# Expert blocks of a mixture layer, laid out over four rounds instead of two

## The chip, the cores and the metric

The kernel runs on one core of a Trainium2 chip. It is one launch of a program in which every engine has its own stream of instructions: TensorE (PE, with its weight loads shown apart as PEld), VectorE (DVE), ScalarE (ACT), GpSimd (POOL) and SyncE (SP). PE does the matrix products, DVE, ACT and POOL the rest of the arithmetic, and SP and POOL issue DMA transfers. Each engine works through its stream in order, and engines wait for each other by semaphores. The metric is the device time of one execution in microseconds, as the median of several runs. All data are 32-bit floats.

## The reference

Four layers are computed on a residual `x` of 4 sequences of 1024 tokens with 128 channels. Every layer has the shape "half a feed-forward step, an attention step, half a feed-forward step". Layers 0 and 2 use a mixture of 8 experts, of which each token takes its best two. Layer 0, cut to what matters (layer 2 has the same form with ReLU, and takes its softmax over the two kept logits):

```python
logits = jnp.einsum('td,ed->te', xf, router_w)
top_vals, top_idx = jax.lax.top_k(logits, K)          # K = 2 of 8 experts
probs = jax.nn.softmax(top_vals, axis=-1)
for e in range(E):
    w = jnp.sum(jnp.where(top_idx == e, probs, 0.0), axis=-1)
    h = jax.nn.gelu(jnp.einsum('td,fd->tf', xf, w1[e]) + b1[e], approximate=False)   # 128 -> 512
    y = jnp.einsum('tf,df->td', h, w2[e]) + b2[e]                                     # 512 -> 128
    out = out + w[:, None] * y
```

The attention of layer 0 works among the 16 heads of each token, that of layer 2 is a causal linear attention. Layers 1 and 3 have no experts.

## The kernel before, in words

**Routing, blocks, passes.** The kernel doesn't compute all experts for all tokens. `route` (L276) normalises a group of sequences, writes their rows to a DRAM tile `rows`, picks two experts for each token, and sorts the pairs of token and expert into blocks of 128 slots, so that all slots of a block have the same expert. It leaves three small tables: `expert` (the expert of each block), `source` (which row of `rows` each slot reads) and `target` (which row of the DRAM tile `res` each slot's result goes to). One sequence makes 23 blocks and two make 39. `experts` (L424) works through the blocks of one group; I call that a pass. `combine` (L476) then reads the two results of each token from `res`, weights them and adds them to the residual, one sequence at a time. Layer 0 has six passes (23, 23, 39, then 39, 23 and 23 blocks, three on either side of its attention), layer 2 has four of 39: 326 blocks in all.

**One block.** For block k the code does this, in the names that the profile shows:

- SP loads the expert's number into a register (L450) and issues one DMA of 578 KB, the expert's up and down matrices and both biases, into a tile `e_w` (L455). Four buffers of it rotate.
- POOL issues an indirect DMA that gathers 128 rows into `e_xg` (L457, six buffers).
- PE transposes them into PSUM (L461; "turn" or T below), and DVE copies the result to `e_x` (L463, three buffers; X).
- Four up products (helper `mm`, L227; U0 to U3), each 128x128, fill one PSUM bank, and after each of them ACT applies the activation with its bias and writes a quarter of `e_h` (L468, three buffers; H).
- Four down products (D) add up in another bank. DVE adds the second bias and writes `e_y` (L441, six buffers; Y). This is the last reader of the block's `e_w`.
- POOL issues an indirect DMA that scatters `e_y` to `res` (L442).

The down half of a block is written behind the up half of the next one: `pending` holds one block back (L469 to L471). So a block spans two rounds of the loop.

**Buffers in PSUM.** [...] In layers 0 and 2 four of them are the pool `main`, four the pool `side`. `experts` takes its three banks per block (turn, up, down) from `main`. A bank that is taken again makes the new writer wait for the last reader of what it held.

**What sets the order.** `experts`, `route`, `combine`, the attentions and the feed-forward steps are Python generators. `macaron` (L1208) puts them into lanes, and `lanes` (L1188) runs the lane that is least far by the costs given at each `yield` (2.6 for a block, 1 at the end of a pass). That fixes only the order in which instructions are written. A scheduler of the framework then orders each engine's stream[...]. The result is fixed when the program is built. In layer 0 the passes stand beside the attention (L501, whose DVE operations on 2048 elements a lane are long) and the routing of later groups; in layer 2 the second and third pass stand beside attention, the first and the fourth nearly alone.

Of the kernel before, what the change touches and what calls it, by code (L numbers as in the profile page):

```python
# [13 lines left out]
ALU = mybir.AluOpType  # L14
AX = mybir.AxisListType

P = 128
B, S, D = 4, 1024, 128
NH, HD = 16, 8
NE, FC = 8, 4  # L20
# [7 lines left out]
MOE_W = 2 * FC * P + FC + D  # L28
# [177 lines left out]
class Macaron:  # L206
# [217 lines left out]
    def experts(self, ps, wp, weights, func, batches, plan):  # L424

        nc = self.nc
        gt = len(batches) * NT
        blocks = blocks_of(gt)
        SP = mybir.EngineType.SP
        rows, source, target, expert = (plan[k] for k in ("rows", "source", "target", "expert"))  # L430
        res = plan["res"] = self.tc.dram_tile([2 * gt * P + blocks * P, D], F32, name=self.name("res"))
        group = self.name("scatter")
        at = lambda ap: bass.IndirectOffsetOnAxis(ap=ap, axis=0)
        bank = lambda shape: self.t(ps, list(shape), "bank")

        def down(k, w, h):
            o = bank((P, D))
            for fc in range(FC):
                self.mm(o, h[:, fc, :], w[:, (FC + fc) * P : (FC + fc + 1) * P], start=fc == 0, stop=fc == FC - 1)
            y = self.t(wp, [P, D], "e_y", bufs=6)  # L440
            nc.vector.tensor_tensor(y, o, w[:, MOE_W - D :], ALU.add)  # L441
            ins = nc.gpsimd.indirect_dma_start(  # L442
                out=res[:, :], out_offset=at(target[:, k : k + 1]), in_=y, in_offset=None
            )
            self.tc.declare_no_dep(ins.ins, group=group, reason="the slots of a group have rows of their own")
            self.tc.add_to_no_dep_group(group, ins.ins)

        pending = None
        for k in range(blocks):
            e = nc.values_load(  # L450
                expert[0:1, k, :], engines=[SP], min_val=0, max_val=NE - 1,
                skip_runtime_bounds_check_because="a count of 8 flags, at most 7",
            )
            w = self.t(wp, [P, MOE_W], "e_w", bufs=4)
            nc.sync.dma_start(out=w, in_=weights[:, bass.ds(e * MOE_W, MOE_W)])  # L455
            xg = self.t(wp, [P, D], "e_xg", bufs=6)
            nc.gpsimd.indirect_dma_start(  # L457
                out=xg, out_offset=None, in_=rows[:, :], in_offset=at(source[:, k : k + 1])
            )
            tp = bank((P, P))  # L460
            nc.tensor.transpose(tp, xg, self.c0["ident"])  # L461
            x = self.t(wp, [P, P], "e_x", bufs=3)
            nc.vector.tensor_copy(x, tp)  # L463
            up = bank((P, FC, P))
            h = self.t(wp, [P, FC, P], "e_h", bufs=3)
            for fc in range(FC):
                self.mm(up[:, fc, :], w[:, fc * P : (fc + 1) * P], x)
                nc.scalar.activation(h[:, fc, :], up[:, fc, :], func, bias=w[:, 2 * FC * P + fc : 2 * FC * P + fc + 1])  # L468
            if pending:  # L469
                down(*pending)  # L470
            pending = (k, w, h)  # L471
            yield 2.6
        down(*pending)
        yield 1

    def combine(self, ps, wp, batches, b, plan):  # L476

# [730 lines left out]
    def macaron(self, name, moe, func, groups, marks, more):  # L1208


        weights, (side, main), wp = self.packs[name + "m"], (self.side, self.main), self.fp
        plans = {}

        def plan(n, group):
            return plans.setdefault((n, group), {"mark": marks[n, group]})

        def route(n, group, *after, ps=side):
            return f"route{n}{group[0]}", after, lambda: self.route(ps, wp, moe, group, plan(n, group))

        def experts(n, group):  # L1220
            names = (f"route{n}{group[0]}",)
            return f"experts{n}{group[0]}", names, lambda: self.experts(main, wp, weights, func, group, plan(n, group))

        def combine(n, group):
            for b in group:
                yield f"combine{n}{b}", (f"experts{n}{group[0]}",), lambda b=b: self.combine(side, wp, group, b, plan(n, group))

        every = [(n, group) for n in range(2) for group in groups[n]]
        blocks = [experts(*g) for g in every]
        back = [task for g in every for task in combine(*g)]  # L1230
        self.lanes(blocks, back, *more(route))
# [140 lines left out]
```

## Time and profile before

The time before is the median of three runs, 3209.11 us (3207.99 to 3214.21). The profile is one execution more, which took 3296.3 us; its span from the first to the last instruction is 3294.4 us, at a mean granted TensorE clock of 0.905.

| stretch, us | what is in it | PE busy | DVE busy | ACT busy | POOL busy | granted clock | GB/s |
|---|---|---|---|---|---|---|---|
| 36 to 145 | layer 0, first pass | 89.56 | 40.30 | 54.44 | 52.22 | 0.78 | 187 |
| 145 to 236 | second pass | 76.81 | 60.34 | 54.12 | 58.68 | 0.94 | 195 |
| 388 to 512 | attention and routing between passes | 52.09 | 93.54 | 29.93 | 0.00 | 0.53 | 45 |
| 512 to 670 | fourth pass | 127.10 | 116.74 | 98.78 | 104.98 | 0.90 | 179 |
| 2129 to 2292 | layer 2, first pass and the routing before it | 140.76 | 50.74 | 70.06 | 84.23 | 0.88 | 192 |
| 2292 to 2452 | second pass | 149.41 | 87.88 | 78.91 | 69.75 | 0.99 | 184 |
| 2480 to 2648 | third pass | 158.50 | 94.11 | 75.25 | 76.02 | 0.96 | 171 |

How to read it: the columns "busy" are the microseconds in which an engine worked inside the stretch, so each is to be held against the stretch's length. A busy PE isn't PE at its peak, since products are pipelined and their ends are modelled. The clock is the share of full speed[...], and GB/s is what the DMA engines moved. In a timeline or a group of instructions, "out<-in" names the tiles written and read, and a bracket or the part behind the last bar gives the idle time of that engine just before, with what ended it. Layers 1 and 3 take most of the rest of the span, 941 to 2129 us and from 2802 us on.

### The profile page before, as it was taken

What the parts mean: (1) busy time and instruction counts of PE and PEld (TensorE: products, weight loads), DVE (VectorE), ACT (ScalarE), POOL (GpSimd) and SP (SyncE); (2) the same over time, 40 slices, a digit from 0 to 9 for tenths busy, and PEclk for the clock granted to TensorE, in tenths of its full rate; (3) what the DMA queues carried; (4) which work ended last, traced back from release to release, by engine and by line L of the source; (5) the groups of instructions that cost most, each with busy time, mean ns of one, the idle gap of its engine ahead of it and who ended that gap; (6) DMA issues with size and microseconds to landing.
All of it is one profiled execution on the core that took longest, in us unless ns stands there. A gap on an engine that the chain in (4) does not pass through costs nothing.

```text
span 3294.4 us, 48535 instructions
## 1 busy us (share of the span) xinstructions
PE 2875.3 (87%) x18206; PEld 1685.8 (51%) x18206; DVE 1826.5 (55%) x3160; ACT 1649.2 (50%) x3640; POOL 807.0 (24%) x748
## 2 busy tenths in 40 slices
PE   6888637878879999999999999988988977899997
PEld 6766426766643333333333333586777865344333
DVE  3376877774226676676776772431555521355664
ACT  3565524658613565566566565444444534444442
POOL 2565405552340000000000000046434454011110
PEclk7989858889977999999999999979989988788997
DMA  4766414663500000000000000157565666000000
GB/s 151 227 186 188 140 42 130 185 188 115 168 9 7 4 6 4 6 6 4 21 5 6 1 1 9 42 152 245 171 185 147 199 197 194 0 0 0 7 7 13
DMA packets 122890, 277.64 MB, mean 84 GB/s; under 512 B 18016, under 2 KB 67296, under 8 KB 122528
## 3 DMA queue, kind: packets, MB, share of 16 engines
q1 hardware_dynamic: 101792, 231.77, 23.8%
q0 software_dynamic: 20864, 42.77, 4.3%
q8 instruction: 144, 2.36, 0.3%
q14 instruction: 90, 0.74, 0.1%
HBM read 238.43 MB, written 31.85 MB: 82 GB/s over the span
## 4 chain that ended last, share of the span: by engine, by line
PE 74%; DVE 12%; ACT 5%; issue 4%; DMA 3%; POOL 1%; another core or an unknown queue 0%; SPq 0%; ACTq 0%; DVEq 0%; POOLq 0%
PE bank L227 40%; PE two L227 17%; PE o L227 8%; PE s L227 4%; DVE nm L720 2%; ACT e_h L468 2%; PE wave L1010 1%; DVE prod L545 1%; PE bank L461 1%; DMA c_y<-res 1%; DVE sc L530 1%; ACT L468 1%; DMA e_w<-in_l0m_dram 1%; DVE prod L528 1%; DVE e_x L463 1%
## 5 line engine op out<-in xcount | busy, mean ns | idle before, releaser
L720 DVE TENSOR_REDUCE nm<-two 128x2 f32<-128x1024 f32 x512 | 626.9, 1225 | 288.3 <-PE s L227 268.9
L743 ACT ACTIVATE e<-s 128x512 f32<-128x512 f32 x1024 | 556.4, 595 | 405.6 <-PE s L227 402.6
L468 ACT ACTIVATE e_h<-bank,e_w 128x128 f32<-128x128 f32 x1304 | 454.8, 368 | 511.6 <-PE bank L227 388.4
L227 PE MATMUL bank<-e_x,e_w 128*128 128x128 f32 x2608 | 569.3, 318 | 154.5 <-ACT e_h L468 79.9
L227 PE MATMUL s<-qm,kz 32*128 32x512 f32 x2048 | 634.1, 643 | 0.8 <-ACT e L743 0.8
L227 PE MATMUL two<-kz,qz 32*128 32x512 f32 x2048 | 593.2, 664 | 21.3 <-DVE nm L720 2.5
L227 PEld LDWEIGHTS bank<-e_x,e_w 128*128 128x128 f32 x2608 | 413.9, 204 | 291.3 <-ACT e_h L468 144.4
L457 POOL DMA_INDIRECT e_xg<-rows,g_source x326 | 334.4, 1026 | 835.1 <-DVE g_target L412 354.2
L227 PE MATMUL bank<-e_w,e_h 128*128 128x128 f32 x2608 | 445.7, 291 | 12.3 <-ACT e_h L468 6.9
L442 POOL DMA_INDIRECT res<-e_y,g_target x326 | 373.5, 1146 | 337.0 <-DVE e_y L441 152.7
L227 PEld LDWEIGHTS bank<-e_w,e_h 128*128 128x128 f32 x2608 | 378.8, 205 | 23.0 <-ACT e_h L468 13.3
L227 PE MATMUL o<-e,va 128*32 128x256 f32 x4096 | 328.8, 392 | 0.1
L441 DVE TENSOR_TENSOR e_y<-bank,e_w 128x128 f32<-128x128 f32 x326 | 94.3, 290 | 403.7 <-PE bank L227 317.0
L227 PEld LDWEIGHTS two<-kz,qz 32*128 32x128 f32 x2048 | 159.7, 189 | 239.9 <-issue 164.0
L227 PEld LDWEIGHTS o<-e,va 128*32 128x32 f32 x4096 | 81.0, 108 | 390.3 <-issue 370.3
L227 PEld LDWEIGHTS s<-qm,kz 32*128 32x128 f32 x2048 | 206.9, 183 | 10.9 <-issue 7.7
L708 POOL COPY va<-vd 128x256 f32<-128x256 f32 x16 | 6.7, 433 | 626.3 <-PE o L227 538.0
L1115 POOL TENSOR_TENSOR z<-st,r 128x512 f32<-128x512 f32 x32 | 46.2, 1445 | 417.1 <-DVE st L1108 333.7
L463 DVE COPY e_x<-bank 128x128 f32<-128x128 f32 x326 | 93.0, 285 | 92.2 <-PE bank L461 67.6
L227 PE MATMUL bank<-g_cols,g_lanes 128*128 128x39 f32 (+1 forms) x512 | 90.5, 341 | 28.9 <-DVE g_cols L392 28.8
L461 PE MATMUL bank<-c,e_xg 128*128 128x128 f32 x326 | 95.0, 291 | 21.7 <-DMA e_xg<-rows,g_source 21.6
L227 PEld LDWEIGHTS bank<-g_cols,g_lanes 128*128 128x128 f32 x512 | 91.2, 270 | 32.5 <-issue 31.4
(300 smaller groups left out, 3694.0 us busy)
## 6 DMA issues: line engine op xcount, KB each, us to landing
e_w<-in_l0m_dram SPq DMA_DIRECT2D x170, 578.0 KB
e_w<-in_l2m_dram SPq DMA_DIRECT2D x156, 578.0 KB
c_y<-res SPq DMA_DIRECT2D x32, 512.0 KB
rows<-g_xt SPq DMA_DIRECT2D x16, 512.0 KB
e_xg<-rows,g_source POOLq DMA_INDIRECT x326
res<-e_y,g_target POOLq DMA_INDIRECT x326
x<-in_x_dram SPq DMA_DIRECT2D x4, 512.0 KB
qz<-qd SPq DMA_DIRECT2D x64, 32.0 KB
```

The costliest lines, as they stand in the source:

```text
L227: self.nc.tensor.matmul(out, lhsT, rhs, start=start, stop=stop)
L441: nc.vector.tensor_tensor(y, o, w[:, MOE_W - D :], ALU.add)
L442: ins = nc.gpsimd.indirect_dma_start(out=res[:, :], out_offset=at(target[:, k : k + 1]), in_=y, in_offset=None)
L457: nc.gpsimd.indirect_dma_start(out=xg, out_offset=None, in_=rows[:, :], in_offset=at(source[:, k : k + 1]))
L461: nc.tensor.transpose(tp, xg, self.c0["ident"])
L463: nc.vector.tensor_copy(x, tp)
L468: nc.scalar.activation(h[:, fc, :], up[:, fc, :], func, bias=w[:, 2 * FC * P + fc : 2 * FC * P + fc + 1])
L528: v.tensor_tensor(pr, q.unsqueeze(2).to_broadcast(sh), k.unsqueeze(1).to_broadcast(sh), ALU.mult)
L530: v.tensor_reduce(sc, pr, AX.X, ALU.add)
L720: v.tensor_reduce(nm[:, it, h, 2 * pair : 2 * pair + 2], s, AX.X, ALU.max, negate=True)
L743: nc.scalar.activation(es[g], s, AF.Exp, scale=scale)
L1115: (pool if i else v).tensor_tensor(z, st[:, 0:HALF], r, ALU.mult)
```

## The change

The body of `experts` is split into four steps, and the loop runs them on four different blocks. In round k it first adds the bias to and scatters block k-3 (`leave`), then loads, gathers, turns and copies block k (`fetch`), multiplies block k-1 up (`up`), and block k-2 down (`down`). So the copy `e_x` is written a round before its products, and the sum of the down products stays in its bank until the next round. The loop has three rounds more, and the weights have five buffers instead of four. What each step issues is the same as before. Lines behind the function stand nine lower in the new file.

```diff
-        def down(k, w, h):
-            o = bank((P, D))
-            for fc in range(FC):
-                self.mm(o, h[:, fc, :], w[:, (FC + fc) * P : (FC + fc + 1) * P], start=fc == 0, stop=fc == FC - 1)
-            y = self.t(wp, [P, D], "e_y", bufs=6)
-            nc.vector.tensor_tensor(y, o, w[:, MOE_W - D :], ALU.add)
-            ins = nc.gpsimd.indirect_dma_start(
-                out=res[:, :], out_offset=at(target[:, k : k + 1]), in_=y, in_offset=None
-            )
...
-        pending = None
-        for k in range(blocks):
+        def fetch(k):
             e = nc.values_load(
...
-            w = self.t(wp, [P, MOE_W], "e_w", bufs=4)
+            w = self.t(wp, [P, MOE_W], "e_w", bufs=5)
             nc.sync.dma_start(out=w, in_=weights[:, bass.ds(e * MOE_W, MOE_W)])
...
             nc.tensor.transpose(tp, xg, self.c0["ident"])
             x = self.t(wp, [P, P], "e_x", bufs=3)
             nc.vector.tensor_copy(x, tp)
-            up = bank((P, FC, P))
+            return k, w, x
+
+        def up(k, w, x):
+            o = bank((P, FC, P))
             h = self.t(wp, [P, FC, P], "e_h", bufs=3)
             for fc in range(FC):
-                self.mm(up[:, fc, :], w[:, fc * P : (fc + 1) * P], x)
-                nc.scalar.activation(h[:, fc, :], up[:, fc, :], func, bias=w[:, 2 * FC * P + fc : 2 * FC * P + fc + 1])
-            if pending:
-                down(*pending)
-            pending = (k, w, h)
-            yield 2.6
-        down(*pending)
-        yield 1
+                self.mm(o[:, fc, :], w[:, fc * P : (fc + 1) * P], x)
+                nc.scalar.activation(h[:, fc, :], o[:, fc, :], func, bias=w[:, 2 * FC * P + fc : 2 * FC * P + fc + 1])
+            return k, w, h
+
+        def down(k, w, h):
+            o = bank((P, D))
+            for fc in range(FC):
+                self.mm(o, h[:, fc, :], w[:, (FC + fc) * P : (FC + fc + 1) * P], start=fc == 0, stop=fc == FC - 1)
+            return k, w, o
+
+        def leave(k, w, o):
+            y = self.t(wp, [P, D], "e_y", bufs=6)
+            nc.vector.tensor_tensor(y, o, w[:, MOE_W - D :], ALU.add)
+            ins = nc.gpsimd.indirect_dma_start(
+                out=res[:, :], out_offset=at(target[:, k : k + 1]), in_=y, in_offset=None
+            )
...
+        held = [None] * 3
+        for k in range(blocks + 3):
+            if held[2]:
+                leave(*held[2])
+            following = fetch(k) if k < blocks else None
+            held = [following, *[step(*x) if x else None for step, x in zip((up, down), held)]]
+            yield 2.6 if k < blocks else 1
```

More of the change, by code (lines that the diff above doesn't have):

```diff
@@ L434, in experts @@
         bank = lambda shape: self.t(ps, list(shape), "bank")
-        def down(k, w, h):
-            o = bank((P, D))
-            for fc in range(FC):
-                self.mm(o, h[:, fc, :], w[:, (FC + fc) * P : (FC + fc + 1) * P], start=fc == 0, stop=fc == FC - 1)
-            y = self.t(wp, [P, D], "e_y", bufs=6)
-            nc.vector.tensor_tensor(y, o, w[:, MOE_W - D :], ALU.add)
-            ins = nc.gpsimd.indirect_dma_start(
-                out=res[:, :], out_offset=at(target[:, k : k + 1]), in_=y, in_offset=None
-            )
-            self.tc.declare_no_dep(ins.ins, group=group, reason="the slots of a group have rows of their own")
-            self.tc.add_to_no_dep_group(group, ins.ins)
-        pending = None
-        for k in range(blocks):
+        def fetch(k):
             e = nc.values_load(
@@ L463, in experts @@
             nc.vector.tensor_copy(x, tp)
-            up = bank((P, FC, P))
+            return k, w, x
+        def up(k, w, x):
+            o = bank((P, FC, P))
             h = self.t(wp, [P, FC, P], "e_h", bufs=3)
             for fc in range(FC):
-                self.mm(up[:, fc, :], w[:, fc * P : (fc + 1) * P], x)
-                nc.scalar.activation(h[:, fc, :], up[:, fc, :], func, bias=w[:, 2 * FC * P + fc : 2 * FC * P + fc + 1])
-            if pending:
-                down(*pending)
-            pending = (k, w, h)
-            yield 2.6
-        down(*pending)
-        yield 1
+                self.mm(o[:, fc, :], w[:, fc * P : (fc + 1) * P], x)
[12 more added lines that the diff above has]
+            )
+            self.tc.declare_no_dep(ins.ins, group=group, reason="the slots of a group have rows of their own")
+            self.tc.add_to_no_dep_group(group, ins.ins)
+        held = [None] * 3
[5 more added lines that the diff above has]
+            yield 2.6 if k < blocks else 1
     def combine(self, ps, wp, batches, b, plan):
```

## The prediction

> **What bounds the kernel now.** I read the page first (busy shares and slices), then the busy time of stretches cut at the passes of expert blocks, then the waits and the timeline of one pass. Only two stretches hold expert blocks: layer 0 (36 to 898 us, 170 blocks) and layer 2 (2129 to 2782 us, 156 blocks). In the built order of both programs every engine's instructions outside these two are the same one by one, so the rest of the span stays.
>
> ```profile
> L468 ACT ACTIVATE e_h<-bank,e_w 128x128 f32<-128x128 f32 x1304 | 454.8, 368 | 511.6 <-PE bank L227 388.4
> L457 POOL DMA_INDIRECT e_xg<-rows,g_source x326 | 334.4, 1026 | 835.1 <-DVE g_target L412 354.2
> L442 POOL DMA_INDIRECT res<-e_y,g_target x326 | 373.5, 1146 | 337.0 <-DVE e_y L441 152.7
> L441 DVE TENSOR_TENSOR e_y<-bank,e_w 128x128 f32<-128x128 f32 x326 | 94.3, 290 | 403.7 <-PE bank L227 317.0
> ```
> Groups of the page: 326 blocks, four activations each, and VectorE stands 403.7 us in front of e_y waiting for PE. Next, two stretches of the table of windows (us, busy PE, PEld, DVE, ACT, POOL, granted clock, DMA share, GB/s), a layer-0 pass beside attention and the last layer-2 pass, which runs nearly alone:
>
> ```profile
> 236.00:388.00 152.00, 118.43 (x718) 96.85 (x718) 117.34 (x174) 93.06 (x215) 91.05 (x72) 0.92 0.58 180
> 2648.00:2782.00 134.00, 104.91 (x684) 86.93 (x683) 27.53 (x103) 60.02 (x172) 76.28 (x79) 0.94 0.71 214
> ```
> No engine is full; the passes are bound by chains. The timeline inside the last pass shows the two links that matter:
>
> ```profile
> 2705.18 0.27 PE L461 MATMUL bank<-c,e_xg 128*128 128x128 f32 x1
> 2705.59 0.28 DVE L463 COPY e_x<-bank 128x128 f32<-128x128 f32 x1
> 2705.93 0.67 PEld L227 LDWEIGHTS bank<-e_x,e_w 128*128 128x128 f32 x4 [0.27 <-DVE e_x L463]
> ...
> 2710.73 0.37 ACT L468 ACTIVATE e_h<-bank,e_w 128x128 f32<-128x128 f32 x1 [0.97 <-PE bank L461]
> 2711.15 0.30 PEld L227 LDWEIGHTS bank<-e_x,e_w 128*128 128x128 f32 x2 [0.81 <-ACT e_h L468]
> 2711.15 0.49 PE L227 MATMUL bank<-e_x,e_w 128*128 128x128 f32 x2 [0.57 <-ACT e_h L468]
> 2711.68 0.37 ACT L468 ACTIVATE e_h<-bank,e_w 128x128 f32<-128x128 f32 x1 [0.58 <-PE bank L227]
> ```
> From a turn (T) to the first up product (U0) that needs its copy (X): 2705.93 - 2705.18 = 0.75 us. From one up product to the next of the same block: 0.53 (2711.15 to 2711.68) + 0.42 (2710.73 to 2711.15) = 0.95 us, because the four share a PSUM bank that ScalarE reads in between. Four such links make a block; PE work must fill them.
>
> [...]
>
> **The change part by part.** Instructions, transfers and their sizes stay: 326 weights, gathers and scatters, 17 products a block; nothing is removed, so all cost lies in order and waits.
>
> *Turn one block ahead.* Before, the built PE order of a lone round is T, U2 of the old block, U0 of the new, U3, D, D, U1, D, D (D: down products). PE issues T in 0.11 us and each product in 0.22 us (two passes 0.11 apart in the timeline), 1.87 us in all. T to U0 has 0.33 us of cover for 0.75: 0.42 lost. U0 to U1 has U0, U3, D, D = 0.88 for 0.95: 0.07 lost; U1 to U2 has 0.77: 0.18 lost. Sum 2.54; the trace's quick rounds are 2.56 us (e_y at 2705.39 and 2707.95). After, the order is T, D, U2, U0, D, D, U3, U1, D; U0 waits for weights only, its copy being a round old. Shortfalls: U2 to U3 0.07, U1 to U2 0.18, with 0.05 for ScalarE's queue: 2.17 us.
>
> *POOL's floor.* A gather start to the scatter start takes 1.27 us and scatter to gather 1.30 (2705.73, 2707.00, 2708.30): 2.57 us a block. So a lone round falls only to 2.57 even where PE would allow 2.17. But the measured mean is 3.04 in the last pass (e_y from 2665.2 to 2780.6, 38 steps): rounds of about 3.5 us come between, until the last gathers have gone, then all are 2.57. In one PE finishes late with no wait that the records name. I can't attribute this 0.45 us; after, PE has 0.40 of slack under POOL's floor to absorb it. Ends: 2.57 (absorbed) and 3.02 (kept); I take 2.7.
>
> *Outputs one block behind.* e_y moves to a later round, so it stands in VectorE's order when its four D are closer to done, and attention queued behind it on VectorE is held less. Between 236 and 388 us VectorE idles 152 - 117 = 35 us; the wait view for 190 to 390 us gives e_y 28.3 and e_x 5.3, that for 500 to 725 us 29.1 and 15.1. I take 40% of these 78 us, ends none and 80%. On the other side D now waits for the copy two blocks ahead and T for e_y four blocks back, since T and D share two of the four banks: a new PE wait with all of PE's queue behind it. Lone, it is covered by a round or more of slack.
>
> *Fifth weight buffer.* Weights are held until e_y, now a round later; the fifth buffer gives that round back. In the last pass a weight transfer takes about 2.4 to 5 us from issue to its last packet in the transfer records, and the up product comes over 6 us after issue. Cost 0; without the buffer SP would issue a round, 2.6 to 4 us, later. SP's order keeps the combine loads behind the same kind of weight loads, one block shifted. POOL puts each scatter one block further behind its gather; six output buffers cover that. At one boundary of layer 2 seven scatters now stand ahead of the next pass's first gather, and its routing result comes only at the last turns: 0 to 5 us, I take 2.
>
> Walking the built PE order with these prices (issue times, plus shortfalls of U links and of T to U0), against the trace from first to last e_y, all us:
>
> | pass (blocks) | measured before | walk before | walk after | gain taken |
> |---|---|---|---|---|
> | L0, first (23) | 85 | 64 | 56 | 8 |
> | L0, second (23) | 86 | 72 | 64 | 8 |
> | L0, third (39) | 144 | 119 | 108 | 14 |
> | L0, fourth (39) | 141 | 114 | 111 | 8 |
> | L0, fifth (23) | 106 | 85 | 85 | 2 |
> | L0, sixth (23) | 84 | 92 | 86 | 6 |
> | L2, first (39) | 122 | 115 | 92 | 15 |
> | L2, second (39) | 154 | 147 | 136 | 9 |
> | L2, third (39) | 159 | 146 | 136 | 9 |
> | L2, fourth (39) | 115 | 120 | 95 | 12 |
>
> The walk meets layer 2 within about 8%; [...]the gains include the VectorE share for the third to fifth passes, kept within 40% of its waits. For the lone passes of layer 2 I take POOL's floor with the 2.7, not the walk: 39 x (3.1 - 2.7) = 15, and 12 where fewer rounds gather. In its second and third, attention products lie in the links (4.44 us a round now, steady); PE work is about 3.8, and one of four links is overlapped: 0.24 a round. Sum 91, less 2 at the boundary: 89 us. Against the profiled execution, 3296.3 us (span 3294.4 and 1.9 around it), that is 3207; the median of the runs is 3209.11, 0.9735 of the profiled one, so 87 us off it: 3122 us.
>
> **Rivals.**
> *Transfers pace the lone rounds.* The 3.02 us is the service time of gathers, weights and scatters together (DMA share 0.71, 214 GB/s in the last pass), and stays. For it: the long rounds end with the last gathers. Against: DMA is not full and no weight wait shows. Then 27 us of layer 2 go and the VectorE share shrinks: gain 20 to 45, about 3175.
> *VectorE stays the pace of layer 0.* Its 117 of 152 us leave little, and only layer 2 gains: 43 us, 3167.
> *Slower: banks couple PE to VectorE.* Place: T and D of layer 0, beside attention's 2.2 us operations. One e_y has 19 VectorE operations ahead of it in the after order, and T two rounds on waits for its bank. Price: one such operation, 2.3 us, uncovered per stalled round. The gain of 87 is used up at 38 stalled rounds of layer 0's 170; at 60 the time is 3209 + 51 = 3260. Against: VectorE's order puts the next copy behind that e_y before the change too.
> *The change does nothing*: ruled out by the built order, unless gains vanish into waits for other lanes: 3209.
>
> **How the numbers follow.** Forecast, gains of 50 to 145 us: 0.58, own range 3065 to 3160. Partial rivals together 0.25 (all faster). No change 0.04; slower 0.13. Tell from no change needs about 0.2%, 6 us. The range 3065 to 3198 leaves out no change and slower, 0.17, above, and 0.03 below.
>
> **What would show it.** Right: the e_x to first-product waits gone, e_y waits well under 317 us, lone layer-2 rounds near 2.6 us with POOL nearly full, the second layer-2 pass near 145 us. Wrong: new waits of PE on e_y or e_x in layer 0; lone rounds at 3.0 us; POOL gathers late at pass starts; a lower clock in layer 0.

## The result and the profile after

The changed kernel takes 3190.3 us (median of 4 runs, 3187.2 to 3191.9), beside 3210.5 us for the kernel before on the same chip: a ratio of 0.9935, with a 95% interval of 0.9918 to 0.9952. It is faster by 20 us, where 87 were forecast, and the time lies inside the range by 8 us. The profiled execution took 3191.45 us (span 3189.6).

The chips were not alike: where the result and the first four experiments were measured the kernel before takes 3209 to 3213 us, on the three chips of the later experiments 3281 to 3291 us. I call them the quick and the long chips, and compare within one kind. By its time the profile before (3296.3 us) belongs with the long ones, though its runs were quick; so I profiled the kernel before once more on the quick chip (3212.5 us, span 3210.7), and the comparison starts from that profile.

First two groups of the page, of the changed kernel (busy us, mean ns | idle before it, what ended it):

```profile
L470 DVE TENSOR_TENSOR e_y<-bank,e_w 128x128 f32<-128x128 f32 x326 | 93.9, 288 | 202.8 <-PE bank L227 189.3
L451 DVE COPY e_x<-bank 128x128 f32<-128x128 f32 x326 | 92.8, 285 | 189.7 <-PE bank L449 178.5
```

The same two groups of the kernel before on the quick chip:

```profile
L441 DVE TENSOR_TENSOR e_y<-bank,e_w 128x128 f32<-128x128 f32 x326 | 94.4, 290 | 335.8 <-PE bank L227 328.1
L463 DVE COPY e_x<-bank 128x128 f32<-128x128 f32 x326 | 92.7, 284 | 83.3 <-PE bank L461 82.0
```

VectorE stands 133 us less in front of e_y, as forecast, but 106 us more in front of e_x. Most of the wait has changed its place.

Next the table of windows (us, busy PE, PEld, DVE, ACT, POOL, granted clock, DMA share, GB/s), for the third pass of layer 0 and the last pass of layer 2. Changed kernel:

```profile
219.00:362.00 143.00, 112.28 (x700) 95.32 (x701) 106.27 (x162) 85.05 (x203) 86.33 (x68) 0.87 0.58 181
2584.00:2676.00 92.00, 87.13 (x644) 78.65 (x642) 24.14 (x86) 51.67 (x156) 65.61 (x67) 0.98 0.85 279
```

Kernel before, profiled again:

```profile
226.00:368.00 142.00, 111.36 (x699) 91.35 (x699) 110.91 (x167) 88.90 (x206) 85.39 (x68) 0.95 0.59 186
2595.00:2698.00 103.00, 95.93 (x644) 79.75 (x643) 22.55 (x87) 55.15 (x156) 66.44 (x68) 0.98 0.79 256
```

The layer-2 pass got 11 us shorter at the same clock; the layer-0 pass beside attention stayed as long as it was, at a lower clock (0.87 instead of 0.95). All passes, from the first to the last e_y on the quick chip, in us:

| pass (blocks) | gain forecast | before, again | after | gain measured |
|---|---|---|---|---|
| L0, first (23) | 8 | 68.3 | 59.2 | 9.1 |
| L0, second (23) | 8 | 92.0 | 84.4 | 7.6 |
| L0, third (39), attention | 14 | 142.1 | 142.5 | -0.4 |
| L0, fourth (39), attention | 8 | 133.4 | 140.0 | -6.6 |
| L0, fifth (23) | 2 | 104.5 | 108.3 | -3.8 |
| L0, sixth (23) | 6 | 79.6 | 80.2 | -0.6 |
| L2, first (39) | 15 | 102.4 | 96.9 | 5.5 |
| L2, second (39), attention | 9 | 155.4 | 150.1 | 5.3 |
| L2, third (39), attention | 9 | 152.2 | 142.5 | 9.7 |
| L2, fourth (39) | 12 | 102.8 | 91.7 | 11.1 |

Layer 2 as a whole, from its first e_y to its last, falls from 568.9 to 537.9 us, a gain of 31.0. Layer 0 grows from 806.7 to 815.8 us, a loss of 9.1: its six passes gain 5.3 together, and the stretches between them lose 14.4. The rest of the span gets 0.8 us longer. That makes up the 21.1 us between the two spans.

Two readings explain the gain of the last pass, and where it ends. A round of the changed kernel in the last pass of layer 2, on VectorE:

```profile
2611.87 0.29 DVE L470 TENSOR_TENSOR e_y<-bank,e_w 128x128 f32<-128x128 f32 x1
2613.69 0.29 DVE L451 COPY e_x<-bank 128x128 f32<-128x128 f32 x1 [1.53 <-PE bank L449]
2614.03 0.29 DVE L470 TENSOR_TENSOR e_y<-bank,e_w 128x128 f32<-128x128 f32 x1
```

and of the kernel before on the quick chip:

```profile
2638.72 0.29 DVE L441 TENSOR_TENSOR e_y<-bank,e_w 128x128 f32<-128x128 f32 x1 [2.07 <-PE bank L227]
2638.92 0.28 DVE L463 COPY e_x<-bank 128x128 f32<-128x128 f32 x1
2641.28 0.29 DVE L441 TENSOR_TENSOR e_y<-bank,e_w 128x128 f32<-128x128 f32 x1 [2.07 <-PE bank L227]
```

Rounds of 2.16 us against 2.56: the walked 2.17 and 2.54. Some 17 such rounds follow each other; then come one of 3.10 and one of 1.97, and from there on they take 2.56 again. POOL's own timeline at that place:

```profile
2636.98 0.99 POOL L471 DMA_INDIRECT res<-e_y,g_target  x1 [0.30 <-issue]
2638.27 0.97 POOL L445 DMA_INDIRECT e_xg<-rows,g_source  x1 [0.30 <-PE bank L227]
2639.54 0.99 POOL L471 DMA_INDIRECT res<-e_y,g_target  x1 [0.30 <-issue]
```

POOL spends 2.57 us a block (2636.98, 2639.54) and falls 0.40 us behind PE in each quick round: its scatter starts 1.6 us after its e_y in the 5th block and 9.4 us after it in the 24th. But that is not what PE waits for. The gathers' lead over their copies falls from about 11 us in the 12th block to about 4 near the end, beside 0.9 to 1.0 us in the first three blocks, and from 2645 us on no wait of PE for a transfer is recorded. What differs is the built order of PE. A late round:

```profile
2645.28 0.27 PE L449 MATMUL bank<-c,e_xg 128*128 128x128 f32 x1
2645.46 0.71 PE L227 MATMUL bank<-e_x,e_w 128*128 128x128 f32 x4
2646.41 0.49 PE L227 MATMUL bank<-e_x,e_w 128*128 128x128 f32 x2 [0.23 <-ACT e_h L459]
2646.73 0.61 PE L227 MATMUL bank<-e_w,e_h 128*128 128x128 f32 x4
2647.18 0.39 PE L227 MATMUL bank<-e_x,e_w 128*128 128x128 f32 x2
2647.40 0.61 PE L227 MATMUL bank<-e_w,e_h 128*128 128x128 f32 x4
2647.85 0.27 PE L449 MATMUL bank<-c,e_xg 128*128 128x128 f32 x1
```

Each product is two passes (the page counts 2608 for the 1304 up products; here each takes 0.27 to 0.38 us, and most neighbours start 0.11 us apart), so I read this as T, U2, U0, U3, D, D, U1, D, D. Nothing but U0 now stands between U2 and U3. With the prediction's prices that link has 0.44 us of cover for 0.95, and U1 to U2 0.77, so the estimate is 1.87 + 0.51 + 0.18 = 2.56 us, which is what the late rounds take. They keep it after POOL's last gather (2661.4 us). Why the built order changes in the later part of the pass was not looked into.

### The profile page after: what moved, and what is told of

Its sections match the earlier page's. It is cut to its first block, busy times and chain, and to the rows that moved or that the text cites. A ratio compares the mean times of both kernels' runs of the same rounds, so it can differ in the third digit from the quotient of the medians.

```text
span 3189.6 us, 48448 instructions
## 1 busy us (share of the span) xinstructions
PE 2823.6 (89%) x18206; PEld 1677.6 (53%) x18206; DVE 1828.0 (57%) x3160; ACT 1633.3 (51%) x3633; POOL 794.8 (25%) x748
## 4 chain that ended last, share of the span: by engine, by line
PE 70%; DVE 8%; ACT 5%; DMA 3%; issue 2%; POOL 1%; ACTq 0%; SPq 0%; POOLq 0%; DVEq 0%
PE bank L227 36%; PE two L227 17%; PE o L227 8%; PE s L227 4%; DVE nm L729 2%; PE wave L1019 1%; ACT e_h L459 1%; DMA c_y<-res 1%; ACT L459 1%; DVE prod L554 1%; PE bank L449 1%; DMA e_xg<-rows,g_source 1%; DVE st L1117 1%; DVE o L556 1%; PE acc L1019 1%
## 5 line engine op out<-in xcount | busy, mean ns | idle before, releaser
L227 PE MATMUL bank<-e_x,e_w 128*128 128x128 f32 x2608 | 538.3, 309 | 85.9 <-ACT e_h L459 50.5
L227 PE MATMUL bank<-e_w,e_h 128*128 128x128 f32 x2608 | 462.4, 293 | 18.4 <-ACT e_h L459 10.3
L471 POOL DMA_INDIRECT res<-e_y,g_target x326 | 358.9, 1101 | 282.4 <-DVE e_y L470 135.9
L227 PE MATMUL bank<-g_cols,g_lanes 128*128 128x39 f32 (+1 forms) x512 | 83.4, 325 | 26.8 <-DVE g_cols L392 25.9
L227 PEld LDWEIGHTS bank<-g_cols,g_lanes 128*128 128x128 f32 x512 | 83.3, 251 | 30.3 <-issue 28.6
```

Of the source, the lines that this page charges most:

```text
L227: self.nc.tensor.matmul(out, lhsT, rhs, start=start, stop=stop)
L471: ins = nc.gpsimd.indirect_dma_start(out=res[:, :], out_offset=at(target[:, k : k + 1]), in_=y, in_offset=None)
```

## The experiments

**The kernel before, once more.** No edit.

> The kernel before, unchanged, profiled once more. Its first profile took 3296.3 us while its runs took 3208 to 3214, and its lone rounds of layer 2 were 2.57 us with longer ones of about 3.5 between. Theory A, that profile was one slow execution: the new one takes 3205 to 3220 us, the fourth pass of layer 2 about 100 us from first to last e_y instead of 115, the long rounds are gone, and layer 2 ends some 60 to 90 us sooner. Theory B, a profile always costs this kernel so much: again about 3296 us, long rounds in the same places. A third, the long rounds are in every execution and the 87 us come from elsewhere: 3210 us with the fourth pass still near 115.

Measured: 3212.5 us. From the first to the last e_y, layer 0 takes 806.7 us, against 837.7 in the first profile, and layer 2 568.9 against 611.8: 74 of the 84 us between the two executions lie in the two stretches that the change touches. In the last pass a round has a median of 2.56 us and a mean of 2.71, not 3.04.

**The parts, one at a time, on the quick chip.** Turning ahead alone, with four weight buffers:

```diff
-        held = [None] * 3
-        for k in range(blocks + 3):
-            if held[2]:
-                leave(*held[2])
+        held = [None] * 2
+        for k in range(blocks + 2):
             following = fetch(k) if k < blocks else None
-            held = [following, *[step(*x) if x else None for step, x in zip((up, down), held)]]
+            fed = up(*held[0]) if held[0] else None
+            if held[1]:
+                leave(*down(*held[1]))
+            held = [following, fed]
```

> Rows turned and copied one block ahead, but each output added and scattered right behind its down products as before, and four weight buffers: one part of the change alone. If the turn is what pays (the 0.42 us from turn to first up product), 3188 to 3195 us, as the whole change. If the late outputs pay (VectorE held less in layer 0), 3205 to 3213. If neither works alone, 3210.

Measured: 3215.7 us, ratio 1.0019 (1.0004 to 1.0034). That is above all three forecasts. Layer 2 gets 19 us shorter and layer 0 24 us longer, mainly because the attention starts 16 us later (first `prod` at 181.1 us instead of 165.3).

Outputs one block behind alone, with four weight buffers:

```diff
-        held = [None] * 3
-        for k in range(blocks + 3):
-            if held[2]:
-                leave(*held[2])
-            following = fetch(k) if k < blocks else None
-            held = [following, *[step(*x) if x else None for step, x in zip((up, down), held)]]
+        held = [None] * 2
+        for k in range(blocks + 2):
+            if held[1]:
+                leave(*held[1])
+            fed = up(*fetch(k)) if k < blocks else None
+            held = [fed, down(*held[0]) if held[0] else None]
```

> Outputs leave PSUM one block behind, but rows are turned and copied in the round of their up products as before, and four weight buffers. If the turn pays alone, 3208 to 3215 us. If the late outputs pay in layer 0, 3190 to 3202. If weights come late without the fifth buffer, since they are held a round longer, above 3220.

Measured: 3210.7 us, ratio 0.9993 (0.9981 to 1.0006), and no pass moves by more than 2.5 us. Alone it does nothing. The time is the one forecast for "the turn pays alone", but the run before shows that the turn alone doesn't.

The whole change without its fifth buffer:

```diff
-            w = self.t(wp, [P, MOE_W], "e_w", bufs=5)
+            w = self.t(wp, [P, MOE_W], "e_w", bufs=4)
```

> The changed kernel with four weight buffers instead of five. If weights are never late, as argued, 3187 to 3194 us. If the fifth buffer carries the change, 3205 us or more, with SP's weight loads a round later and waits of up products on them.

Measured: 3198.7 us, ratio 0.9958 (0.9944 to 0.9972), some 8 us above the change with five. The loss is the last pass of layer 2, 99.9 us instead of 91.7, in which PE's weight loads now wait for `e_w` 9 times, 5.0 us in all; with five buffers they don't. Layer 0 is 4.3 us *shorter* than with five, to which I come back.

Taken together: in layer 2 the first three passes get their gain from the turn alone (98.3, 150.0 and 142.2 us, within 1.4 us of the whole change), and the last one, 102.5 with the turn alone, gets most of it from the fifth buffer. In layer 0 the turn alone loses 24 us, the turn with late outputs 4.8. So the late outputs, which do nothing alone, are worth some 20 us there beside the turn (one execution each).

**The layout in one layer only, on a long chip.** `experts_two` is the old function:

```diff
-            return f"experts{n}{group[0]}", names, lambda: self.experts(main, wp, weights, func, group, plan(n, group))
+            return f"experts{n}{group[0]}", names, lambda: (self.experts if name == "l2" else self.experts_two)(main, wp, weights, func, group, plan(n, group))
```

> The new layout in layer 2 alone (five weight buffers there); layer 0 keeps the layout of before with four. Against the second profile of before, the changed kernel leaves layer 0 about 10 us later and gains about 31 us in layer 2. Theory L, the two layers' parts add up: about 3212 - 31 = 3181 us, faster than the changed kernel by 8 to 12. Rival, the loss in layer 0 is chance of one profile or comes from elsewhere: 3190 as the changed kernel.

> The new layout in layer 0 alone, layer 2 as before. Theory L: 3212 + 10 = 3222 us, the first pass some 9 us shorter, the attention stretches of layer 0 longer by 3 to 6 us each. Rival, layer 0 gains as was forecast, 46 us, and only the profile hid it: 3170 to 3180.

Measured: in layer 2 alone 0.9997 (0.9980 to 1.0013), in layer 0 alone ("l0" in place of "l2" above) 1.0125 (1.0093 to 1.0158), with the kernel before at 3291 us. On this chip the layout costs 41 us in layer 0 and gains nothing that can be measured in layer 2.

**The copy e_x on ScalarE in layer 0**, in the changed kernel and in the kernel before, on the same chip:

```diff
-            nc.vector.tensor_copy(x, tp)
+            (nc.scalar.copy if func == AF.Gelu else nc.vector.tensor_copy)(x, tp)
```

> The changed kernel with the copy of the turned rows done by ScalarE instead of VectorE in layer 0 (170 copies of 285 ns off VectorE, and the chain from the turn over the copy to the down product's bank no longer through VectorE's queue). If VectorE paces layer 0 in the attention stretches (77 copies there, 22 us), layer 0 gets 15 to 40 us shorter: 3150 to 3175. If the pace of layer 0 is the order of PE's stream, not VectorE: 3185 to 3200.

> The kernel before with the same copy on ScalarE in layer 0, the control. If VectorE's load is the pace whatever the layout, it gains as much as the changed kernel does by this edit: 3170 to 3195. If the new layout's bank coupling through VectorE is what costs layer 0, the control gains clearly less than the changed kernel does: 3200 to 3212.

Measured: 1.0088 (1.0057 to 1.0118) and 1.0077 (1.0046 to 1.0107). In the kernel before the move costs 0.8%. The changed kernel with it is no better than the changed kernel alone against its own control on long chips (1.0065 to 1.0079, below). Moving 170 copies from VectorE to ScalarE does not free layer 0. Since ScalarE takes them over (45 us in all), this doesn't tell whether VectorE's load is the pace; the quarter below does more.

**The change, its layer-2 part, and layer 2 with the first pass, on a long chip.** The second kernel is the one-layer kernel above; the third also gives the new layout to the first pass of layer 0:

```diff
+            return f"experts{n}{group[0]}", names, lambda: (self.experts if name == "l2" or (n, group) == (0, (0,)) else self.experts_two)(main, wp, weights, func, group, plan(n, group))
```

> The changed kernel once more, for its parts on the same chip. Theory L (the layout gains about 31 us in layer 2 and loses about 10 in layer 0, where the attention on VectorE sets the pace): 20 us under the kernel before, ratio 0.993, where the kernel before takes about 3210 us. Theory T (PE's pauses, not the chain of turn and copy, set the lone rounds on a chip where the kernel before takes about 3290 us): there its lone rounds stay near 3.0 us and the ratio is about 1.01.

> The new layout in layer 2 alone, layer 0 as before. Theory L: layer 2 keeps its 31 us and layer 0 loses nothing, ratio 0.990 where the kernel before takes about 3210 us. Rival (the gain of layer 2 belongs to the order of both layers together): no better than the whole change, 0.993 or above. Theory T, where the kernel before takes about 3290 us: 1.000.

> The new layout in layer 2 and in the first pass of layer 0, which runs before any attention; the other five passes of layer 0 as before, with five weight buffers. Theory L: the first pass ends 8 us earlier, the first sequence's attention starts with it and nothing after it is held up: 5 to 8 us under the layout in layer 2 alone, ratio 0.988. Rival (the gain of the first pass is given back at the start of the second, whose routing is held): equal to the layout in layer 2 alone.

Measured, with the kernel before at 3284.7 us: 1.0079 (1.0056 to 1.0102), 0.9984 (0.9963 to 1.0004) and 1.0007 (0.9991 to 1.0024). So the change that is 20 us faster on the quick chip is 21 us slower on this one. The split explains it: leaving layer 0 as it was takes the loss away, 26 us by the medians here. The first pass of layer 0 gives no gain either, as the rival said: it ends 3 us earlier, but the second pass then starts 7 us later and takes 94.0 us instead of 85.1. (The two profiled executions are the shortest of the one kernel and the longest of the other, so the 94.0 may be in part chance.) None of the split kernels was run on the quick chip; there I estimate 31 us for the layer-2 part, from its share of the whole change.

What the lone rounds of a long chip look like shows in the timeline of the last layer-2 pass of the changed kernel there:

```profile
2700.97 0.27 PE L449 MATMUL bank<-c,e_xg 128*128 128x128 f32 x1
2702.09 0.63 ACT L459 ACTIVATE e_h<-bank,e_w 128x128 f32<-128x128 f32 x2 [1.72 <-PE bank L449]
2702.21 0.29 DVE L451 COPY e_x<-bank 128x128 f32<-128x128 f32 x1 [3.22 <-PE bank L449]
2702.51 0.49 PE L227 MATMUL bank<-e_w,e_h 128*128 128x128 f32 x2 [1.26 <-ACT e_h L459]
```

VectorE's copy starts 1.24 us after the turn, where it was 0.41 us in the prediction's timeline; ScalarE's activation starts at nearly the same moment, 0.12 us before the copy, and PE goes on only 1.54 us after the turn. That is one pause. The weights of the median block had landed 6.6 us before its first activation, and its gather 14.6 us before its copy. In this pass 11 pairs of neighbouring PE starts lie over 1.0 us apart, 15.1 us in sum; in the same pass on the quick chip there is 1. The kernel before has 9, 13.0 us in sum, in the prediction's own profile and 1 on the quick chip. That is most of the 0.45 us a round that the prediction could not attribute.

**Half of the weight traffic left out**, on the same chip:

```diff
+            if k % 2 == 0:
+                e = nc.values_load(
...
+                shared[0] = self.t(wp, [P, MOE_W], "e_w", bufs=5)
+                nc.sync.dma_start(out=shared[0], in_=weights[:, bass.ds(e * MOE_W, MOE_W)])
+            w = shared[0]
```

> The changed kernel with one weight transfer for every two blocks: the odd block multiplies with the matrices of the even one before it, so half of the weight traffic is left out. If weight transfers pace lone rounds, the median round of the fourth pass of layer 2 falls where the changed kernel shows about 3.0 us, and the late part of that pass, which shows 2.56 us on another chip, falls too. If PE's own pauses or POOL's gathers and scatters (2.57 us a block) do, the rounds stay as they are in the changed kernel on the same chip, within 0.1 us.

Measured: 3295.8 us (one run). The windows of the last pass of layer 2, first of the changed kernel, then of this one:

```profile
2670.00:2784.00 114.00, 93.33 (x638) 80.29 (x636) 23.56 (x86) 52.24 (x155) 65.52 (x68) 0.96 0.70 225
```

```profile
2672.00:2783.00 111.00, 91.54 (x648) 81.84 (x646) 25.07 (x86) 51.38 (x156) 65.57 (x68) 0.96 0.42 130
```

Traffic falls from 225 to 130 GB/s, the mean round only from 2.98 to 2.89 us, and the 11 pauses stay (15.6 us). The median falls from 2.56 to 2.26, so the weights touch the rounds between the pauses; the pauses are not theirs (one execution). The gathers are not ruled out: in this pass the last pause comes near the last gather, 2761.9 and 2760.2 us in the changed kernel, 2763.4 and 2761.3 in this one, 2758.6 and 2760.1 in the profile before, while in the first and the last of these weights go on being issued for some 10 us more without a pause. No run leaves gathers out. What the pauses are stays open.

**What holds layer 0: function tables or VectorE?** Both kernels, on a long chip, with another activation in layer 0:

```diff
-        self.macaron("l0", moe, AF.Gelu, groups, marks, more)
+        self.macaron("l0", moe, AF.Relu, groups, marks, more)
```

> The kernel before with ReLU in place of Gelu in the experts of layer 0 (another function is computed). The trace shows 120 loads of ScalarE's function tables in layer 0, of 1.28 us each, 53 of them at the experts' activations. Theory A (these loads in the chain from product to activation to product hold the rounds of layer 0): layer 0 gets 40 us shorter or more, here and in the changed kernel alike or more there. Theory V (VectorE's attention sets layer 0's pace): under 25 us.

> The changed kernel with ReLU in place of Gelu in the experts of layer 0 (another function is computed). Theory A: without the loads the new layout gains in layer 0 what was forecast beside attention, 20 to 30 us, so this kernel is that much better against the kernel before with ReLU than the change is against the kernel before with Gelu. Theory V: no such difference; layer 0 stays about 10 us longer than with the old layout.

and with a quarter of the attention's arithmetic on VectorE:

```diff
+        Q = NH // 4
...
-            sh = [P, NH, NH, HD]
+            sh = [P, Q, NH, HD]
...
-            sh = [P, NH, HD, NH]
+            sh = [P, Q, HD, NH]
```

> The kernel before with a quarter of the VectorE arithmetic of layer 0's attention: scores and sums for 4 of the 16 heads, the rest filled by a copy (so three quarters of that attention are left out). Theory V: VectorE sets the pace of layer 0, so layer 0 gets 60 us shorter or more. Theory A or banks: under 40 us.

> The changed kernel with the same quarter of layer 0's attention on VectorE (three quarters left out). Theory V: with VectorE out of the way the layout gains in layer 0, so against the kernel before with the quarter it is 20 us or more better than the change is with the whole attention. Rival, the rounds' own coupling of banks: layer 0 stays about as far behind the old layout as with the whole attention, 10 us or more.

Measured, with the kernel before at 3281.0 us: ReLU 3251.1 and 3276.5, the quarter 3206.8 and 3215.4. The table loads exist; in the kernel before they stand at the experts' activation as

```profile
L468 ACT ACT_TABLE_LOAD x56 | 71.8, 1283 | 5.1 <-PE bank L227 3.4 <-issue 0.8
```

and with ReLU this line is gone, and of 120 loads in layer 0 there are 24 left. At the attention's exponential (L535) 27 loads become 5, each still of 1283 ns, and the experts' activations take 368 ns in the mean with either function. Removing the loads is worth some 30 us to both kernels (the changed one took 3306 us with Gelu on this chip), and the changed kernel stays 25 us behind the old layout, as with Gelu (21 to 26). They are a cost of layer 0, and not the cause asked for.

The quarter gives the kernel before 74 us, over the 60 that meant "VectorE sets the pace", and the changed kernel is then 8.6 us behind, not 21 to 26. So 12 to 17 us of its loss go with VectorE's work, less than the 20 forecast, and some loss stays. The two have 5 and 6 runs, the second from 3206 to 3225 us, so these figures are good to several us only.

**One product of the attention written earlier**, from a reading of the traces that the next section shows. A handover is the time from the last `prod` of VectorE in one attention sequence to the first in the next:

```diff
-            yield 11.2
             if k == 3:
                 y = bank()
                 self.mm(y, m["wfc"], oS)
                 c = slice((i - 3) * P, (i + 1) * P)
                 v.tensor_tensor(X[:, c], X[:, c], y, ALU.add)
+            yield 11.2
```

> The changed kernel, as the measure for the next one on the same chip. Its handovers between attention sequences (last VectorE product of one to the first of the next) take 31 to 35 us for the first and third, as in the other traces of it; against the kernel before 0.993 on a chip where that takes about 3210 us, 1.008 where it takes about 3285 us.

> The changed kernel with one step of layer 0's attention written earlier: the product with the output weights and its addition to the residual stand before the yield of their tile, not behind it, so that in the built order of PE 3 products of experts, not 35 to 40, stand between the last turn of a sequence and that product. Theory H (the held product makes VectorE's attention start late, and with it all of layer 0): the first and third handover lose about 7 us each, layer 0 ends 10 to 16 us earlier, and the kernel is 10 to 16 us faster than the changed kernel on the same chip, 0.3 to 0.5%. Rival (the handover only moves a wait that VectorE meets elsewhere): within 4 us of the changed kernel.

Measured, with the kernel before at 3284.0 us: 1.0065 (1.0044 to 1.0086) and 1.0067 (1.0037 to 1.0097). No gain; the forecast of 10 to 16 us failed. The reason is in its timeline, where the product (into a bank, from oS) now comes at once, and the next step of the same chain comes 14 us later:

```profile
307.91 0.27 ACT L575 COPY oS<-bank 128x128 f32<-128x128 f32 x1 [0.19 <-issue]
308.43 1.02 PE L227 MATMUL bank<-oS,l0a 128*128 128x512 f32 x2
309.49 0.69 DVE L580 TENSOR_TENSOR x<-x,bank 128x512 f32<-128x512 f32 x1 [0.79 <-issue]
323.18 1.02 PE L227 MATMUL bank<-x,c 128*128 128x512 f32 x2
```

The edit moved the hold one product along. The first and third handover took 36.6 and 41.1 us, and 35.5 and 38.4 in the changed kernel on that chip.

## Why the prediction was right or wrong

**What bounds the kernel: the base of the sum failed.** The forecast summed durations of an execution 84 us above the runs, and scaled the gain by 0.9735, as if that difference lay evenly over the span. It lay, 74 of 84 us, in the expert stretches. The rounds of the last pass were 2.71 us in the mean on the quick chip, not 3.04.

**Turn one block ahead: right where the walked order stands.** Walked 2.54 to 2.17, measured 2.56 to 2.16. (The old round's sum leaves out the link from U2 to U3, with 0.86 us of cover for 0.95; with it U0 to U1 loses nothing, and the sum is 2.56.) PE's waits for `e_h`, in which these links show beside the down products' own, come to 52.6 us in 72 waits over layer 0 of the kernel before and 53.1 in 65 of the changed one. But the prediction gives this one order for a lone round, and the late rounds have another. In the last pass the turn pays only with the fifth buffer. In layer 0 the turn alone loses 24 us. The two attention passes of layer 2, where 0.24 us a round was forecast for the overlapped link (9 and 9 us), gave 5.3 and 9.7.

**POOL's floor: wrong as a floor, and the pace of the late rounds is not shown to be POOL's.** POOL does take 2.57 us a block. But 18 rounds run below that, on the lead of the gathers, and in the late rounds, which take 2.56, PE waits for ScalarE in an order of its own (3.0 us in 13 waits for `e_h` between 2645 and 2676 us, 0.5 in 2 between 2612 and 2645) while the gathers have landed about 4 us ahead. That the two figures agree was taken for a mechanism. The two lone passes of layer 2 gained 5.5 and 11.1 us where 15 and 12 were taken: the base left less room.

**The 0.45 us with no named wait: not absorbed.** I let PE's slack take most of it. On the quick chip most of it isn't there: the mean of 2.71 us owes what it has over 2.56 to the first rounds of the pass. On a long chip it stays in the changed kernel (mean 2.98 us in the last pass). It is for the most part the pauses of PE. Half of the weight traffic did not remove them, so of the rival "transfers pace the lone rounds" the weights are out, and its observation that the long rounds end with the last gathers still stands.

**Outputs one block behind, 40% of 78 us in layer 0: this step failed**, and layer 0 is most of the miss: 46 us forecast, a loss of 9 measured, so 55 of the 67 us missed. The step treated waits of VectorE as time to be saved, 31 us of them. The outputs alone left layer 0 at 806.1 us instead of 806.7; beside the turn they only take back what the turn costs there, a cost that the prediction put at nothing. The view of waits over layer 0, of the changed kernel (us in total, times, longest):

```profile
PE bank L227 <- DVE e_x L451: 27.2, 9, 7.4
...
DVE e_y L470 <- PE bank L227: 106.9, 69, 6.0
DVE e_x L451 <- PE bank L449: 77.9, 55, 5.2
```

and of the kernel before on the quick chip:

```profile
PE bank L227 <- DVE e_x L463: 25.9, 25, 2.5
...
DVE e_y L441 <- PE bank L227: 144.1, 92, 3.6
DVE e_x L463 <- PE bank L461: 46.3, 34, 5.5
```

VectorE's two expert waits go from 190.4 to 184.8 us: most of what left e_y came back at e_x. PE waits for e_x 9 times instead of 25, but as long in sum, so "e_x to first-product waits gone" did not come true.

What layer 0's length follows is one lane of work on VectorE, the attention of four sequences, one after another: in the five traces of the quick chip layer 0 ends 174 to 178 us after the lane's last `prod`. From the first to the last product `prod` of each, on the quick chip, in us:

| | start | seq. 0 | handover | seq. 1 | handover | seq. 2 | handover | seq. 3 | end |
|---|---|---|---|---|---|---|---|---|---|
| before, again | 165.3 | 109.2 | 25.3 | 100.5 | 16.0 | 119.4 | 27.7 | 123.2 | 686.5 |
| after | 160.0 | 107.7 | 31.5 | 99.5 | 18.2 | 120.5 | 34.4 | 123.7 | 695.5 |

The sequences take as long as before, within 1.5 us. The first passes' gain shows as a start 5.3 us earlier; the first and third handover then lose 12.8, and the lane ends 9.0 us later, as layer 0 does (9.1 us longer). Inside such a handover, in the changed kernel:

```profile
279.62 0.27 PE L574 MATMUL bank<-c,o 128*128 128x128 f32 x1
279.93 0.27 ACT L575 COPY oS<-bank 128x128 f32<-128x128 f32 x1 [0.19 <-PE bank L574]
288.23 1.02 PE L227 MATMUL bank<-oS,l0a 128*128 128x512 f32 x2
```

and in the kernel before:

```profile
282.13 0.27 PE L565 MATMUL bank<-c,o 128*128 128x128 f32 x1
282.44 0.27 ACT L566 COPY oS<-bank 128x128 f32<-128x128 f32 x1
282.75 1.13 PE L227 MATMUL bank<-oS,l0a 128*128 128x512 f32 x2
```

The product with the output weights starts 0.05 us after its input is there in the one and 8.0 us after it in the other, with no wait of PE in between: PE works through 31 products and 4 turns of experts that stand ahead of it in the built order. The built order has 1 expert instruction in this place before the change and 35 after, at the ends of sequences 0 and 2 alike, and 1 against 40 at the end of sequence 3. Why they stand there was not looked into.

How far is this shown? Four weight buffers on the same chip give a first measure. There the built order has 2 in these two places, so the hold is gone. The handovers take 27.3 and 31.8 us, 4.2 and 2.6 less than with five, and layer 0 is 4.3 us shorter, but still 4.8 us longer than in the kernel before. The two differ in more than the hold (with four the lane starts 5.7 us later), and each is one execution, so this is no clean test. But about half of the loss is there without the hold.

Handovers don't add to the layer one for one, either. With a quarter of the attention the new layout has 106 and 36 in these places, and the handovers take 51.5 and 72.4 us, beside 28.5 and 32.4 in the old layout with 7 and 8. Yet layer 0 is only 7.1 us longer, since its sequences take 43 us less in sum. And the one experiment that was to remove the hold only moved it, so that lifting it brings the loss back was not shown.

A rival stands untested. The prediction named a lower clock in layer 0 as a sign of being wrong, and it is there: the mean over layer 0 is 0.87 in the kernel before, 0.83 in the changed one and 0.85 with four buffers. Whether it costs time or follows from the gaps in PE's work, no run separates.

So the lane's account is measured, the hold is seen, and the rest of the loss stays open. On long chips the same account, against the kernel with the old layer 0, gives 19 of a 30 us loss to the handovers; the rest is not settled there.

**Fifth weight buffer, cost 0: right**, and it is needed: 8 us, nearly all in the last pass of layer 2. That it also changes the built order (35 expert instructions in each of the two places in front of the attention's product, 2 with four buffers) was not foreseen; layer 0 is 4.3 us longer with it. Four buffers in layer 0 with five in layer 2 were not tried.

**The boundaries: 2 us was right for layer 2 (0.7), and layer 0's had no term.** They cost 14.4 us, by the handovers and by the second pass, which starts 13.1 us after the first one's end instead of 3.4.

**The rivals.** "VectorE stays the pace of layer 0", 3167, came nearest: only layer 2 gains, though less than 43. It didn't foresee that layer 0 could lose. "Slower" named the banks, and e_y; the waits of PE's products for e_y in layer 0 are only 6.4 us, 4.5 before. In the handovers PE is late without any recorded wait, by its order. On the long chips, slower is what happened.

## What to carry to other kernels

Before working out a gain from a profile, hold its time against the runs: where it differs by more than the runs' spread, find the stretch that holds the difference, since it may be the one that the change is about. In a program whose order is fixed when it is built, a change to one lane can put its work ahead of another lane's (here 35 expert instructions where 1 had been, and a product that starts 8.0 us after its input); look in the built order for what now stands in front of the lane that sets the pace, for the views of waits need not name it. And when a stretch runs at the pace of a floor that was worked out, look whether the engine waits there: here PE's own order gives the same 2.56 us. Parts tried alone don't add up either: the late outputs did nothing alone, and beside the turn they saved some 20 us in layer 0.

## What the runs showed of the hardware

The same program took 3213 us on one chip and 3281 to 3291 us on three others. By its two profiles, 3212.5 and 3296.3 us, 74 of the 84 us lie in the stretches that hold expert blocks. In the last pass of layer 2 on a long chip the starts of neighbouring PE products lay 1.0 to 1.6 us apart (once 2.6) 11 times in a pass of 39 blocks, with the median block's weights landed 6.6 us and its gather 14.6 us before their use, and as often with half of the weight traffic. The passes beside the attention of layer 2 on the same chip show 1 or 2 such pauses. The cause is not known. I had taken the runs and the profile of one kernel to be of one kind. The sign of this change depended on it: 0.9935 on the one chip, 1.0065 to 1.0079 on the others.
